# Softmax totals spread by way of DRAM, and the next sequence's last tiles normalised at other points, in an attention and top-1 LoRA block

## The chip, the cores and the metric

The kernel runs on one core of a Trainium2 chip. The metric is the device time of one execution in microseconds (us); lower is better. Before the change, three runs took 2750.57, 2753.59 and 2754.35 us, a median of 2753.59. One more execution was profiled; all traces and instruction times come from it.

The core's engines run their own instruction streams in order and wait for each other by semaphores: TensorE (PE, matmuls; its weight loads are listed apart as PEld), VectorE (DVE), ScalarE (ACT), GpSimd (POOL) and SyncE (SP). Every transfer of this kernel is issued on SP, in one order; an issue that waits holds back all issues behind it.

## What is computed

Four sequences of 1024 tokens with 1024 features, in fp32. One pre-norm block of attention with 32 heads of 32 features, then one pre-norm block that routes each token to the best of eight experts, each a LoRA pair of rank 16:

```python
def attn(x):                      # x is the layer norm of the input
    q, k, v = (split_heads(x @ w) for w in (wq, wk, wv))
    q, k = rotary(q), rotary(k)
    scores = einsum('bqhd,bkhd->bhqk', q, k) / sqrt(32)
    scores = where(causal, scores, lowest)
    return merge(softmax(scores) @ v) @ wo

def ffn(x):                       # x is the layer norm of what attention left
    logits = x @ route_w.T
    value, index = top_k(logits, 1)
    gate = one_hot(index, 8) * value
    h = einsum('bsd,erd->bser', x, A)
    return einsum('bser,eor->bso', gate[..., None] * h, Bw)

x = x + attn(layernorm(x))
x = x + ffn(layernorm(x))
```

## The kernel before

**Units.** The work is cut into 32 units u, one for each sequence b and each group g of four heads (128 columns of wq, wk, wv). A unit has 16 query tiles t of 64 queries; tiles 0 to 7 are its block 0, tiles 8 to 15 its block 1. While the scores of unit u are computed, the projections of unit u+1 are made and, from the second sequence on, one 128-token tile of the sequence before is finished: projected by wo, added, normalised, routed, and sent through its expert (`finish_steps`).

**Filling.** The program is written in the order that the engines take it. A list `SLOTS` gives a unit 11 slots: nine score rounds and two marks, "second" and "first", where the values are applied. Between the slots the steps waiting in `todo` are emitted, `do_some`, each with a cost; a step of cost 1 is one 128x512 matmul. The share of a slot is `ahead[r] / sum(ahead[r:ends_at])` (L1076 to L1081), where `ahead` is the list `LENGTHS` in units 0 to 6 and all ones later. `do_postponed` (L226) counts the cost of emitted steps and runs a postponed piece of work once its cost is used up.

**A score round** (`score_round`, L393) makes scores in PSUM for the query tiles of the slot (L406). There is one PSUM tile for this, `s` of the pool `ps_s`, and the value product uses the same one (L554). ScalarE copies the scores out (L417), GpSimd masks the diagonal (L420), DVE finds the maxima (L438), combines them (L459), ScalarE exponentiates with the sums (L467), and DVE transposes the probabilities in 32x32 squares (L492).

**Totals and values.** The keys of one query lie in two quarters of the partitions. `join_sums` (L525) runs when a block's probabilities are all transposed: four additions of a quarter and its partner (L534), one reciprocal of 128x16 (L535), and on GpSimd a copy that repeats each reciprocal 32 times (L537), so that `by` has 128x512 numbers with the queries on partitions. `apply` (L981) then multiplies probabilities and values on PE (L573), 64 or 128 matmul pairs, in one piece for block 0 and in two for block 1; between two pieces other steps are emitted and DVE transposes the value tile (`meanwhile`, L1028). `spread_sums` (L542) transposes `by` on PE with four matmuls (L547) and copies the result back on ScalarE (L548). `scale_values` multiplies the product by `by` on DVE (L593), which frees the PSUM tile for the next score round, and a later slot stores it to a DRAM scratch (L606). The mark "second" applies block 1 of the unit before, the mark "first" block 0 of the unit at hand. `join_sums` of block 1 comes in slot 1, that of block 0 in the rounds between the marks.

**Transfers.** Weights of the projections arrive in `w` (two buffers, L218), the values go to DRAM and come back in another layout (L507, L513), and wo, router and LoRA weights come as chunks (L647) into four buffers, the next three always ahead of the one in use.

**Change of sequence.** In units 7, 15 and 23 the next sequence's eight token tiles are loaded, normalised and transposed between other steps, by a `Norm` (L233): `load`; `find` (moments, L172 to L182: two BN_STATS, an aggregate, an addition on DVE and a power on GpSimd); `scale` (L186 on DVE); `turn` (eight PE transposes L198, two ScalarE copies L200 and L202). `change_steps` (L789) writes out by hand where tiles 2 to 7 stand among the steps of the last unit. For the second sequence, tiles 0 to 3 are turned in the steps of unit 6 and the rest in those of unit 7, all from buffers of the tag `row`; `scale(t)` there also finds the moments of tile t+1 (L270). For the third and fourth sequence not all tiles have a `row` buffer: tile 3 is loaded into the new unit's qT, tile 4 into its kT and tile 6 again into qT (L839), each before its rotary result is written there.

## Time and profile before

| what | value |
|---|---|
| median of three runs | 2753.59 us |
| the profiled execution's own time | 2747.7 us |
| its span, first to last instruction | 2745.9 us |
| mean granted TensorE clock | 0.998 |
| transfers | 317.86 MB, 16 DMA engines busy 41.6% on the kernel's queue |
| spreadings of totals (L547, four matmuls each) | 64 |
| reciprocals (L535) | 64, 253 ns each |
| products scaled (L593) | 128, 417 ns each; DVE idle before them 158.1 us in all |
| start of the first spreading, and of the last | 108.2 us, 2691.9 us |

A line of the groups reads: line, engine, operation, out<-in with their shapes, count | busy time and mean duration | idle time of that engine just before, and what ended it. Durations of neighbouring matmuls overlap, because they are pipelined: what one of them costs is the distance from start to start. In a timeline, a line is: start, duration, engine, line, operation, out<-in, count, and in brackets the idle time before it. Idle time of an engine which no other engine waits for costs nothing.

The waits of PE, longest sums first (us in total, times, longest):

```profile
PE pt_a L198 <- DVE x L186: 9.8, 2, 9.1
PE s L406 <- ACT pr L417: 7.2, 6, 1.7
PE pt_a L198 <- ACT yn L200: 5.2, 2, 2.6
PE pt_a L198 <- DVE qT L186: 4.5, 2, 2.3
PE po L690 <- DMA chunk<-in_wo: 4.0, 5, 1.7
```

The first of them is the start of the kernel, where the first tile is loaded and normalised. The chain of work that ended last lies for four fifths on PE:

```profile
PE 80%; DVE 14%; ACT 2%; DMA 1%; POOL 1%; issue 1%; SPq 0%; POOLq 0%; DVEq 0%; ACTq 0%
```

### The profile page before, as it was taken

The page shows a single profiled execution, that of the slowest core. Times are in us where ns is not written, and L with a number is a line of the kernel's source. Part 1 is how long each engine was busy: PE and PEld are TensorE (multiplying, and loading weights), DVE is VectorE, ACT ScalarE, POOL GpSimd, SP SyncE. Part 2 cuts the span into 40 slices and gives each one's busy share as a digit, 9 for nine tenths or more (in the row PEclk, how much of TensorE's full clock was granted, in tenths as well). Part 3 has the DMA queues.
Part 4 walks back from the last instruction along what each step waited for, and adds up shares of the span by engine and source line. Part 5 has one row for each costly group of instructions (what it writes and reads, how often), then busy time and mean ns, then how long its engine had stood idle before and what let it go on. Part 6 is the DMA issues. An engine that isn't in the chain of part 4 may idle for free.

```text
span 2745.9 us, 84082 instructions
## 1 busy us (share of the span) xinstructions
PE 2682.2 (98%) x35328; PEld 1322.0 (48%) x35328; DVE 2126.7 (77%) x4198; ACT 1755.0 (64%) x5033; POOL 638.1 (23%) x900
## 2 busy tenths in 40 slices
PE   8999999899999999989999999998999999999998
PEld 5444444444445444445444454444544444544445
DVE  4888889887777877887777778788777777778655
ACT  2877777876666676666666666666566666666521
POOL 2222223222222222222222222222222222222000
PEclk9999999999999999999999999999999999999999
DMA  3222232325444455551654444565255544446421
GB/s 118 52 56 56 56 94 56 78 56 150 131 135 114 121 141 142 151 171 43 175 145 122 135 110 121 149 165 146 63 157 150 138 128 128 115 119 196 129 67 55
DMA packets 448012, 317.86 MB, mean 116 GB/s; under 512 B 150289, under 2 KB 371729, under 8 KB 447633
## 3 DMA queue, kind: packets, MB, share of 16 engines
q1 hardware_dynamic: 447632, 312.47, 41.6%
q8 instruction: 278, 4.55, 0.7%
q14 instruction: 102, 0.83, 0.1%
HBM read 262.59 MB, written 49.81 MB: 114 GB/s over the span
## 4 chain that ended last, share of the span: by engine, by line
PE 80%; DVE 14%; ACT 2%; DMA 1%; POOL 1%; issue 1%; SPq 0%; POOLq 0%; DVEq 0%; ACTq 0%
PE po L690 14%; PE pq L313 14%; PE pk L313 13%; PE pv L313 12%; PE s L406 11%; PE av L573 9%; DVE top L438 4%; DVE pr L492 4%; PE ph L712 2%; PE pf L751 2%; DMA chunk<-in_wo 1%; DVE both L459 1%; PE pr L547 1%; ACT pr L417 1%; PE pt_f L198 1%
## 5 line engine op out<-in xcount | busy, mean ns | idle before, releaser
L467 ACT ACTIVATE pr<-pr,both 128x256 f32<-128x256 f32 (+15 forms) x2048 | 1045.1, 519 | 58.0 <-DVE both L459 57.9
L438 DVE TENSOR_REDUCE top<-pr 128x2 f32<-128x960 f32 (+15 forms) x768 | 651.1, 894 | 251.5 <-POOL pr L420 250.9
L417 ACT COPY pr<-s 128x640 f32<-128x640 f32 (+14 forms) x544 | 525.3, 1017 | 492.3 <-PE s L406 491.7
L492 DVE STREAM_TRANSPOSE pr<-pr 128x1024 f32<-128x1024 f32 (+11 forms) x768 | 664.3, 907 | 33.3 <-ACT pr L467 30.1
L420 POOL TENSOR_TENSOR pr<-pr,causal_sb 128x128 f32<-128x128 f32 x512 | 238.0, 472 | 1070.6 <-ACT pr L417 1062.4
L313 PE MATMUL pv<-xnT,wv 128*128 128x512 f32 x1024 | 484.1, 600 | 0.0
L313 PE MATMUL pq<-xnT,wq 128*128 128x512 f32 x1008 | 476.8, 600 | 0.6 <-ACT xnT L200 0.6
L313 PE MATMUL pk<-xnT,wk 128*128 128x512 f32 x1008 | 475.9, 601 | 0.0
L406 PE MATMUL s<-kT,qT 32*32 32x256 f32 (+4 forms) x17408 | 393.0, 385 | 10.7 <-ACT pr L417 7.2
L467 ACT ACTIVATION_READ_ACCUMULATOR pr<-pr,both 128x1 f32 x2048 | 400.8, 196 | 0.0
L690 PE MATMUL po<-chunk,attn 128*128 128x512 f32 x736 | 376.3, 597 | 4.0 <-DMA chunk<-in_wo 4.0
L406 PEld LDWEIGHTS s<-kT,qT 32*32 32x32 f32 x17408 | 187.2, 103 | 267.2 <-issue 101.8
L313 PEld LDWEIGHTS pk<-xnT,wk 128*128 128x128 f32 x1008 | 181.3, 190 | 234.8 <-issue 234.6
L313 PEld LDWEIGHTS pq<-xnT,wq 128*128 128x128 f32 x1008 | 182.6, 191 | 224.0 <-issue 221.8
L313 PEld LDWEIGHTS pv<-xnT,wv 128*128 128x128 f32 x1024 | 185.7, 190 | 217.2 <-issue 212.9
L573 PE MATMUL av<-pr,vals 64*32 64x256 f32 (+3 forms) x12288 | 273.2, 320 | 11.7 <-DVE pr L492 11.6
L573 PEld LDWEIGHTS av<-pr,vals 64*32 64x32 f32 x12288 | 215.5, 106 | 119.9 <-issue 54.5
L459 DVE TENSOR_TENSOR both<-top 32x4 f32<-32x4 f32 (+3 forms) x1152 | 213.4, 185 | 23.7
L690 PEld LDWEIGHTS po<-chunk,attn 128*128 128x128 f32 x736 | 135.2, 190 | 168.0 <-issue 149.6
L548 ACT COPY by<-pr 128x512 f32<-128x512 f32 x64 | 37.5, 586 | 260.5 <-PE pr L547 260.5
L593 DVE TENSOR_TENSOR at<-av,by 128x256 f32<-128x256 f32 x128 | 48.1, 417 | 158.1 <-ACT by L548 158.0
L690 PE MATMUL po<-wo,attn 128*128 128x512 f32 x256 | 116.7, 597 | 0.0
(87 smaller groups left out, 1705.8 us busy)
## 6 DMA issues: line engine op xcount, KB each, us to landing
chunk<-in_wo SPq DMA_DIRECT2D x368, 256.0 KB, 3.6
vals<-vd SPq DMA_DIRECT2D x256, 128.0 KB, 4.5
x<-in_x SPq DMA_DIRECT2D x58, 512.0 KB, 6.0
wq<-in_wq SPq DMA_DIRECT2D x32, 512.0 KB, 4.0
wk<-in_wk SPq DMA_DIRECT2D x32, 512.0 KB, 4.0
wv<-in_wv SPq DMA_DIRECT2D x32, 512.0 KB, 4.2
vd<-vT SPq DMA_DIRECT2D x128, 128.0 KB, 4.8
out_y<-x SPq DMA_DIRECT2D x32, 512.0 KB, 2.8
```

Of the source, the lines that this page charges most:

```text
L313: nc.tensor.matmul(at["p"], lhsT=wt[:, c, :], rhs=xnTs[b, tb][:, c, :], start=(c == 0), stop=(c == NC - 1),)
L406: nc.tensor.matmul(sc[i * SQ : (i + 1) * SQ, h, at : at + w].rearrange("p (j k) -> p j k", k=SQ), lhsT=of_q[rows, 2 * t + half], rhs=of_k[ ...
L417: nc.scalar.copy(pr[:, :, k0 : k0 + w], sc[:, :, at : at + w])
L420: nc.gpsimd.tensor_tensor(diagonal, diagonal, causal_sb.unsqueeze(1).to_broadcast([P, HG, SQ]), ALU.add)
L438: nc.vector.tensor_reduce(top[:, k, h : h + step], places[u, t][:, h : h + step, :], AX.X, ALU.max, negate=True,)
L459: nc.vector.tensor_tensor(dst[rows], src[rows], src[other], op)
L467: nc.scalar.activation(pr[:, h, :], pr[:, h, :], AF.Exp, bias=tops[u, t][:, h : h + 1], accum_out=dens[u, t // QT][:, t % QT, h : h + 1],)
L492: nc.vector.transpose(pr, pr)
L573: nc.tensor.matmul(avs[half][h * HD : (h + 1) * HD, t0:, :], lhsT=v[rows, j, h * HD : (h + 1) * HD], rhs=rhs, start=(j == 0), stop=(j == n ...
L690: nc.tensor.matmul(st["po"], lhsT=lhsT, rhs=rhs, start=(c == start), stop=(c == stop))
L712: nc.tensor.matmul(ph, lhsT=st["ynT"][:, c, :], rhs=w[:, c - i * RA, :], start=(c == 0), stop=(c == NC - 1),)
L751: nc.tensor.matmul(pf, lhsT=st["whT"], rhs=rhs, start=True, stop=True)
```

## The change

It has two parts.

*Totals.* `join_sums` writes the additions and the reciprocal into a constant tile `rec_sb` with 32 columns for each block (the unused ones are zeroed once), transposes it in 32x32 squares on DVE, and sets up two pieces of work, `put` and `get`. `put` stores four pieces of 16 rows x 32 numbers to a DRAM tile in which the 512 reciprocals of a head lie one after the other; `get` loads for each of the four heads its 512 numbers 32 times, once for each partition of the head in `by`. They are postponed by 2.0 and 5.0 of emitted cost; `spread_sums` runs what is left of them. GpSimd's copy, the four PE transposes and ScalarE's copy are gone.

*Changes of sequence.* For the second sequence (units 6 and 7), `scale` finds the next moments only for tiles 0 to 3, and the steps of unit 7 turn tile 4 after four projection steps, tile 5 after nine, then find, scale and turn tiles 6 and 7, the last of them after step 15. Unit 7 fills its slots by `LENGTHS`, but with 6.5 for each of the first two slots. For the third and fourth sequence tile 2 is turned one projection step and one held step later, tile 6 is loaded into kT when tile 4 has been turned, and tiles 5 to 7 are found, scaled and turned after other steps than before.

```diff
+LONG = 6.5
...
+    rec_sb = const.tile([P, 2, SQ], F32, name="rec_sb")
+    nc.vector.memset(rec_sb, 0.0)
...
-                if self.b == 1:
+                if self.b == 1 and k < TB:
                     self.find(k + 1)
...
-        den = dens.pop((u, blk)).rearrange("p (t c) h -> p c t h", c=2)
-        rec = small.tile([P, TB, HG], F32, tag="rec", name=f"rec_{u}_{blk}", bufs=2)
+        den = dens.pop((u, blk)).rearrange("p (t c) h -> p c h t", c=2)
+        rec = rec_sb[:, blk, : HG * TB].rearrange("p (h t) -> p h t", t=TB)
...
-        nc.vector.reciprocal(rec, rec)
-        bys[u, blk] = by = big.tile([P, TB, P], F32, tag="by", name=f"by_{u}_{blk}")
-        nc.gpsimd.tensor_copy(
-            by.rearrange("p t (h d) -> p t h d", d=HD),
-            rec.unsqueeze(3).to_broadcast([P, TB, HG, HD]),
-        )
+        nc.vector.reciprocal(rec_sb[:, blk, : HG * TB], rec_sb[:, blk, : HG * TB])
+        turned = small.tile([P, SQ], F32, tag="recT", name=f"recT_{u}_{blk}", bufs=2)
+        nc.vector.transpose(turned, rec_sb[:, blk])
+        there = dram.tile([HG * TB, P // SQ, SQ], F32, tag="recs", name=f"recs_{u}_{blk}")
+        by = big.tile([P, TB * P], F32, tag="by", name=f"by_{u}_{blk}")
+
+        def put():
+            for i in range(P // SQ):
+                nc.sync.dma_start(there[:, i], turned[i * SQ : i * SQ + HG * TB])
+
+        def get():
+            for h in range(HG):
+                of_h = there[h * TB : (h + 1) * TB]
+                nc.sync.dma_start(
+                    by[h * HD : (h + 1) * HD],
+                    bass.AP(of_h.tensor, of_h.offset, [[0, HD], [1, TB * P]]),
+                )
+
+        left = [put, get]
+        bys[u, blk] = by, left
+        for cost in (2.0, 5.0):
+            postponed.append([cost, lambda: left and left.pop(0)()])
...
-        by = bys.pop((u, blk))
-        pt = bank([P, TB, P], f"pr_{u}_{blk}")
-        for i in range(TB):
-            nc.tensor.transpose(pt[:, i, :], by[:, i, :], eye_sb)
-        nc.scalar.copy(by, pt)
-        return by.rearrange("p t k -> p (t k)")
+        by, left = bys.pop((u, blk))
+        while left:
+            left.pop(0)()
+        return by
...
-            out += [*h[:2], turn, *h[2:4], find(3), p[0], h[4], turning(2), h[5], p[1], route, scaling(3)]
+            out += [*h[:2], turn, *h[2:4], find(3), p[0], *h[4:6], p[1], turning(2), route, scaling(3)]
...
-            out += [p[6], find(5), p[7], turning(3), scaling(5), *p[8:10], turning(4), *p[10:12]]
-            chains = weave(chains[:-6], p[12:]) + chains[-6:]
-            out += [*chains[:2], find(6), *chains[2:4], scaling(6), turning(5), *chains[4:6], find(7)]
-            out += [*chains[6:8], scaling(7), turning(6), *chains[8:14], turning(7)]
-            return out + chains[14:]
-        out += [*chains[:2], turning(4), scaling(6), *chains[2:6], turning(5), scaling(7)]
-        out += [*chains[6:11], turning(6), *chains[11:16], turning(7)]
+            out += [p[6], find(5), p[7], turning(3), scaling(5), *p[8:10], turning(4)]
+            chains = weave(chains[:-6], p[10:]) + chains[-6:]
+            out += [*chains[:5], turning(5), find(6), *chains[5:7], scaling(6), *chains[7:9], find(7)]
+            out += [chains[9], turning(6), *chains[10:12], scaling(7), *chains[12:15], turning(7)]
+            return out + chains[15:]
+
+        out += [*chains[:4], turning(4), *chains[4:9], turning(5), *chains[9:11], norm.finding(6)]
+        out += [*chains[11:13], scaling(6), chains[13], norm.finding(7), chains[14], scaling(7)]
+        out += [turning(6), chains[15], turning(7)]
...
-                norm = Norm(b + 1, {0: (2,), 2: (5,), 3: (6,)}, {3: "q", 4: "k", 6: "q"})
+                norm = Norm(b + 1, {0: (2,), 2: (5,), 4: (6,)}, {3: "q", 4: "k", 6: "k"})
...
-            ahead = LENGTHS if not b and u + 1 < NG else [1.0] * ends_at
+            ahead = [1.0] * ends_at
+            if not b:
+                ahead = LENGTHS if g + 1 < NG else (LONG, LONG, *LENGTHS[2:])
```

In the steps of `change_steps`, `chains` are the projection steps of the next unit, `p` the wo steps of the tile that is finished, `h` the held last projection steps of the unit at hand, `turn`, `route`, `turn_hidden` and `adapt` the later stages of a finished tile.

## The prediction

> **What bounds the kernel now.** I read the engine totals first, then the windows of 50 us, the group of each instruction that goes, the waits of TensorE (PE), and last the timeline around the places that the change touches. Units are numbered u0 to u31, eight to a sequence; "apply (u, 0)" and "apply (u, 1)" are the value products of a unit's two blocks, each followed by one spreading of totals, 64 in all.
>
> ```profile
> PE 2682.2 (98%) x35328; PEld 1322.0 (48%) x35328; DVE 2126.7 (77%) x4198; ACT 1755.0 (64%) x5033; POOL 638.1 (23%) x900
> ...
> 200.00:250.00 50.00, 48.71 (x783) 23.11 (x782) 39.75 (x81) 37.56 (x117) 15.63 (x20) 1.00 0.28 65
> 1000.00:1050.00 50.00, 50.00 (x776) 25.98 (x774) 38.99 (x76) 30.80 (x91) 10.19 (x17) 1.00 0.41 107
> 1150.00:1200.00 50.00, 46.93 (x691) 25.62 (x691) 47.36 (x97) 35.02 (x93) 12.59 (x21) 1.00 0.51 160
> ...
> L547 PE MATMUL pr<-eye_sb,by 128*128 128x128 f32 x256 | 42.2, 287 | 0.9 <-issue 0.9
> ...
> PE av L573 <- DVE pr L492: 11.6, 2, 9.1
> ```
>
> The columns of a window are its stretch, its length, busy PE, weight loads, VectorE (DVE), ScalarE, GpSimd, clock, DMA share. From about 600 us on PE has no gap at all in most windows: there a PE instruction that goes is worth its time. In the first sequence PE idles about 1 us in 50 and DVE is close behind. At the changes of sequence (1150 and again 1850) DVE has 47 of 50 us and PE idles. The largest single wait, 9.1 us, stands at the first change, in u7.
>
> **The transposes that go (L547, with GpSimd's L537 and ScalarE's L548).** The steady unit, on PE, DVE and SP:
>
> ```profile
> 1028.64 3.68 PE L573 MATMUL av<-pr,vals 64*32 64x256 f32 x128
> 1035.03 2.35 PE L573 MATMUL av<-pr,vals 64*32 64x256 f32 x128
> 1037.31 0.66 PE L547 MATMUL pr<-eye_sb,by 128*128 128x128 f32 x4
> 1037.80 1.02 PE L690 MATMUL po<-chunk,attn 128*128 128x512 f32 x2
> ...
> 1027.98 0.25 DVE L535 RECIPROCAL rec<-rec 128x16 f32<-128x16 f32 x1
> 1038.67 0.76 DVE L593 TENSOR_TENSOR at<-av,by 128x256 f32<-128x256 f32 x2 [2.99 <-ACT by L548]
> ...
> 1020.13 8.98 SPq L647 DMA_DIRECT2D chunk<-in_ra  x3
> 1038.86 2.19 SPq L647 DMA_DIRECT2D chunk<-in_wo  x4
> ```
>
> The durations overlap, so I take starts: four transposes hold PE from 1037.31 to 1037.80, 0.49 us, and not 4 x 0.287. All 64 would be 31.4 us. ScalarE's 37.5 us (64 copies of 586 ns) and GpSimd's 39.1 us lie beside PE's work and are put at nothing; L593 waited for that copy, but ends 3.75 us before PE's next score round.
>
> **What takes their place.** One DVE transposition of 128x32, four stores of 2 KB, four loads of 64 KB, all on SP's queue; loads wait for the stores to land, and everything that SP issues later waits too. The smallest transposition in the trace, 128x128, takes 304 ns and 128x256 401, so 128x32 is estimated at 0.25; it falls into DVE's idle time before L593 (1.2 to 3 us) and costs nothing, as does one memset at the start, ahead of the first x. On SP the first of a row of issues takes 0.33 us, the next 0.45, so the fourth starts 1.35 after the first. For the landing the trace bounds both ends:
>
> ```profile
> chunk<-in_ra SPq DMA_DIRECT2D x24, 136.0 KB, 2.2
> vals<-vd SPq DMA_DIRECT2D x256, 128.0 KB, 4.5
> vd<-vT SPq DMA_DIRECT2D x128, 128.0 KB, 4.8
> ```
>
> Both new kinds are smaller than any of these, so I take the row nearest in packets, the first: 0.25 + 1.35 + 2.2 + 1.35 + 2.2 = 7.4 us from the reciprocal to the spread tile. The slow rows give 0.25 + 1.35 + 4.8 + 1.35 + 4.5 = 12.3. A trip faster than 7.4 gains only in u0, below.
> The Trainium skill, "DMA: Bandwidth & Descriptors", section "Bandwidth", speaks against such traffic: it counts transfers under 64 KB as dominated by descriptors. Its section "Anatomy of one DMA" has a fixed 2.0 us and bytes at 436 GB/s (measured from GpSimd's queue); with these the trip is an estimated 7.1 us, and the sum below would end 0.3 us better; the 2.2-us row decides.
>
> **Last three sequences.** In the steady unit the product ends 9.1 us after the reciprocal (1028.23 to 1037.31) in block 1, 9.3 in block 0. A trip of 7.4 is hidden; even at 12.3 L593 would end 13.1 after the reciprocal, and the next score round, which needs its PSUM, starts at 1043.18, that is 14.5 after it once 0.49 is gone. So 0.49 counts in full. What SP holds back: as built, in block 1 the stores stand before the second router load (ra) and the loads of totals before the third, and they wait for a reciprocal that ends at 1028.23, where SP before issued the third ra load at 1028.74. Stores are out at 1030.2, ra 2 follows at once, totals' loads at 1032.4 to 1034, ra 3 at 1034.2, landing 2.2 later at 1036.4; PE wants it at about 1039.4. In block 0 two weight chunks slip by 4 to 5 us and are used 13 and 18 us after the reciprocal: hidden. If this cover were gone, PE would wait at L712 or L690. Exceptions are the first block of u16 and u24, where a chunk is wanted 5.2 us after the reciprocal and lands at 1.9 + 3.6 = 5.5: 0.3 lost, twice. Sum: of the 48 spreadings, four are at changes of sequence; 44 x 0.49 = 21.6, less 0.6, is **21.0 us**.
>
> **First sequence.** Here DVE sets part of each unit:
>
> ```profile
> 238.08 0.25 DVE L535 RECIPROCAL rec<-rec 128x16 f32<-128x16 f32 x1
> 243.72 2.37 DVE L492 STREAM_TRANSPOSE pr<-pr 128x1024 f32<-128x1024 f32 x2
> 246.01 0.72 DVE L593 TENSOR_TENSOR at<-av,by 128x256 f32<-128x256 f32 x2
> 279.89 0.76 DVE L593 TENSOR_TENSOR at<-av,by 128x256 f32<-128x256 f32 x2 [2.78 <-ACT by L548]
> ```
>
> In block 0 L593 starts without idle time, 7.7 us after the reciprocal, inside a stretch in which DVE is busy from 239.5 to 277 and releases the next product; PE's 0.49 there becomes a wait. A trip of 7.4 just fits; each us above 7.7 is lost once per unit. In block 1 PE sets the pace, 0.49 counts, and L593 would have to start later than 10.4 after the reciprocal to hurt. So u1 to u6 give 6 x 0.49 = 2.9. In u0 the reciprocal ends at 106.78 and L593 starts at 109.54: no lead. With 7.4 it starts at 114.2, 4.7 us later, and DVE, which then runs without a pause to the next product at 135.18, carries that on: **-4.7**. First sequence without u7: **-1.8**.
>
> **Change of sequence, u7.** Before, tiles 6 and 7 are normalised ahead of the last probability transpositions (ended 548.6), for which PE waits from 539.0:
>
> ```profile
> 543.24 0.81 DVE L186 TENSOR_SCALAR x<-x,mv_a,rstd_a 128x1024 f32<-128x1024 f32 x1
> 543.97 1.28 DVE L175 BATCH_NORM_STATS2 st_a<-x 128x6 f32<-128x512 f32 x2
> ...
> 548.09 5.90 PE L573 MATMUL av<-pr,vals 64*32 64x256 f32 x128 [9.05 <-DVE pr L492]
> ...
> 543.00:548.00 5.00, 0.00 (x0) 0.00 (x0) 4.88 (x11) 4.70 (x17) 1.80 (x4) 0.50 0.01 2
> ```
>
> The wait is 9.05 us, and the clock fell to half, so the product took 5.90 instead of 3.68. After: the moments of 6 (1.7), scaling of 6 (0.8) and moments of 7 (1.7), 4.2 us, come behind; and LONG puts 6 more steps of 0.9 us ahead of the product. DVE waited 3.4 us at L593 near 514, of which 2.2 go, and the score round at 527.5 moves up as much; so the transpositions end near 548.6 - 4.2 - 2.2 = 542.2, and PE arrives near 539.0 - 2.2 + 5.4 = 542.2: no wait. But tile 6 is now turned between the two pieces of the product. DVE needs after the transpositions 1.0 (totals), 0.25, 2.9 (maxima L438, L459), 1.5 (swap), 1.7 (moments of 6), 1.2, 1.2 (vT), 0.8 (scaling), 10.6 us; PE has 3.7 + 1.8 = 5.5 us of work: a new wait of 5.1 us. PE alone gains 9.05 + 2.2 + 1.0 (two spreadings) - 5.1 = 7.1; but DVE arrives at the next score round only some 5 us early, and it follows PE closely to the end of the unit. I take **+5.5**, with 1 to 11 as ends (1 if the clock falls again and DVE holds the rest, 11 if the new wait closes).
> The Trainium skill, "TensorE: Matmul & The Clock Gate", section "What's actually happening", halves the clock after one idle window of about 3.4 us; by it the 5.1-us wait would cost an estimated 1.7 us more. The trace is not so clean: a gap of 2.60 us before 135.18 was followed by a window with clock 0.66, one of 2.60 at 1182 by none.
>
> **Changes at u15 and u23.** PE waits 2.6 (second tile), 0.5, 0.7, 1.6 (a chunk) and 2.3 (tile 6 in qT), 7.6 us each. The first is moved past the score round, but DVE ends the transpositions for the product at 1194.2 either way, so PE waits there instead. SP now holds three chunks, issued at 1190.3 to 1191.5 before, behind stores that wait for the reciprocal at 1195.23; the first is issued near 1197 and lands at 1199.5 to 1200.6 where PE wants it at 1197.9: 2 to 3 us lost. Later the 1.6 goes, since no projection step stands there any more, and the 2.3 shrinks to nothing or stays, because tile 6's load now waits for tile 4's turn and stands behind the value stores. I take **+1.1** each with their two spreadings, ends -4 and +4.
>
> **Sum.** 21.0 - 1.8 + 5.5 + 2.2 = 26.9, say 27. The profiled execution, 2747.7 (span 2745.9), would become 2720.7; it lies 5.9 below the median of the runs, 2753.6, which becomes **2726.6**.
>
> **Rivals.**
> *A slow trip, faster all the same.* At 10 us, between the rows, block 0 of u1 to u7 loses 7 x 2.3 = 16 and u0 another 2.6: gain 8, 2745. For it: the stores are 128-byte rows, like those of vd. Against: vd has 64 times as many, and DMA share is 0.28 in this stage. Chance 0.17.
> *A trip so slow that the first sequence pays for everything.* At 12.3 us block 0 loses 7 x 4.6 = 32, block 1 7 x 1.9 = 13, u0 4.9 more: 27 - 50 = 23 slower, 2777. It decides from 10.7 us on (21 + 2 + 3.3 lost, against 27); slower by 0.2% from 11.1. For and against it: as above. Chance 0.08.
> *More than forecast.* The wait at tile 6 closes, the changes of sequence give +4 each, block 0 of the first sequence counts too (3): 27 + 5.5 + 5.8 + 3 = 41, 2712. DVE, shown as full there, speaks against it. Chance 0.15.
> *The change doesn't do what it says*, the trip lying open behind every product: only u0 is built so, where stores and loads are issued right beside the product; elsewhere they come 6 to 9 us ahead.
>
> **How the numbers follow.** Forecast 0.60, with its own range 2718 to 2736 from the ends of the changes of sequence. The range for 8 in 10, 2712 to 2745, takes in the third rival and the first up to its value. A measurement of this kernel tells 0.2%, 5.5 us, from no change. Slower by that: the second rival, 0.08; within it: 0.06 of the first rival, trips of 10.4 to 11.1; faster: the rest, 0.60 + 0.15 + 0.11 = 0.86.
>
> **What would show it.** PE starts within 0.1 us of each product's end with a projection step; a steady unit shortens by 0.99 us from 82.33 (995.75 to 1078.08 for the spreading of block 0). The spread tile lands 7 to 8 us after the reciprocal. In the first sequence L593 of block 0 has no wait for a DMA except in u0, of some 7 us. In u7 the 9.1 us is gone and a wait at L198 of about 5 stands. At u15 PE waits for a wo chunk behind the first piece. Waits of L690 or L712 for chunks in steady units would prove me wrong, and so would L593 waiting on the totals' DMA in every unit.

## The result and the profile after

Predicted were 2726 us, with 2712 to 2745 as the range. Measured, 14 executions each on one chip: before 2750.8 us, after 2751.0 us (medians); ratio 1.0001, 95% interval 0.9993 to 1.0008. The change moved nothing that can be measured; the forecast of 27 us faster was wrong. The profiled execution of after took 2748.2 us (span 2746.4), that of before 2747.7. Among the executions of the variants below, one of `totals_alone` took 7545 us and stands in no ratio.

Line numbers below are those of the kernel named. In after, the join's additions are L539, the reciprocal L540, the transposition L542, the stores L548, the loads L553, the product L592, its scaling L612, a score round L410, the maxima L442 and L463, the turn of a tile L202 (copies L204, L206), its scaling L190, its moments L179 to L183, the value stores L511, tile 6's load L260, projections with wo L709, the router product L731. A kernel with lines added has its later lines as much further down.

From the page: engine total of PE, and the two new kinds of transfer with their size and median time from issue to landing.

```profile
PE 2672.7 (97%) x35072; PEld 1303.2 (47%) x35072; DVE 2146.2 (78%) x4263; ACT 1719.2 (63%) x4969; POOL 599.8 (22%) x836
...
by<-recs SPq DMA_DIRECT2D x256, 64.0 KB, 2.1
...
recs<-recT SPq DMA_DIRECT2D x256, 2.0 KB, 1.4
```

The 256 transpositions are gone and PE's busy time is 9.5 us less, while the span is 0.5 us longer: PE idles 10 us more. The waits of PE, of which the start of the kernel is 9.3 us, say where (us in total, times, longest):

```profile
PE pt_a L202 <- DVE x L190: 20.4, 5, 9.3
PE pt_a L202 <- DVE kT L190: 9.4, 2, 4.8
PE s L410 <- DVE at L612: 8.7, 3, 4.0
PE ph L731 <- ACT xnT L204: 7.6, 2, 4.1
```

The second and the fourth are new, the first has three more waits than before, and the third was 2.3 us in 2 there. The first two are turns of tiles at changes of sequence (and the start), the third are scalings that come late for a score round, the fourth is the router product at u15 and u23.

Where the time went is read best from one event that both kernels have 64 times, the start of the scaling of a product (L593 before, L612 after). After minus before, in us, from the two traces:

| scaling in | after − before | stretch up to it |
|---|---|---|
| u0, block 0 | +4.1 | lost |
| u4, block 1 | −3.5 | regained, and 0.4 for each spreading |
| u5, block 0 | +1.3 | 4.8 lost |
| u6, block 0 | 0.0 | partly regained |
| u7, block 1 | −4.1 | 4.1 gained at the first change |
| u14, block 0 | −9.0 | 4.9 gained, evenly |
| u15, block 1 | −0.3 | 8.6 lost at the second change |
| u22, block 0 | −5.2 | 4.8 gained, evenly |
| u23, block 1 | +3.2 | 8.3 lost at the third change |
| u30, block 0 | −2.2 | 5.4 gained, evenly |
| end of the span | +0.5 | 2.7 lost from there on |

Even gains in the steady units, and two falls at u15 and u23 that take back more than half of them. In detail, the steady unit, on PE, DVE and SP (start, duration, engine, line, operation, names, shapes, count, idle before):

```profile
1028.18 2.35 PE L592 MATMUL av<-pr,vals 64*32 64x256 f32 x128
1030.46 1.13 PE L709 MATMUL po<-chunk,attn 128*128 128x512 f32 x2
...
1021.18 0.25 DVE L540 RECIPROCAL rec_sb<-rec_sb 128x16 f32<-128x16 f32 x1
1030.59 0.76 DVE L612 TENSOR_TENSOR at<-av,by 128x256 f32<-128x256 f32 x2 [1.52 <-PE av L592]
...
1021.71 1.72 SPq L548 DMA_DIRECT2D recs<-recT  x4
1024.49 2.48 SPq L553 DMA_DIRECT2D by<-recs  x4
```

The scaling starts 0.06 us behind the product and waits for nothing else: the trip is hidden. But the pair of wo projections behind the product takes 1.13 us where it took 1.02 behind the transpositions, so 0.10 of the 0.49 us came back: a steady unit is 0.78 shorter, not 0.99. In before, the weight load of the first of the two starts at 1037.70, 0.11 ahead of its matmul at 1037.80, beside the last transposition; in after both start at 1030.46.

The second change of sequence, u15; the first line is the turn of tile 6 in before, the others are of after:

```profile
1228.94 1.06 PE L198 MATMUL pt_a<-eye_sb,qT 128*128 128x128 f32 x8 [2.26 <-DVE qT L186]
...
1223.14 1.94 PE L202 MATMUL pt_a<-eye_sb,kT 128*128 128x128 f32 x8 [4.60 <-DVE kT L190]
...
1234.94 1.87 PE L202 MATMUL pt_a<-eye_sb,x 128*128 128x128 f32 x8 [2.83 <-DVE x L190]
...
1216.66 2.35 DVE L442 TENSOR_REDUCE top<-pr 128x2 f32<-128x1024 f32 x2 [4.19 <-POOL pr L424]
1219.04 0.66 DVE L463 TENSOR_TENSOR both<-top 32x4 f32<-32x4 f32 x4
1219.73 1.29 DVE L179 BATCH_NORM_STATS2 st_a<-kT 128x6 f32<-128x512 f32 x2
1222.18 0.81 DVE L190 TENSOR_SCALAR kT<-kT,mv_a,rstd_a 128x1024 f32<-128x1024 f32 x1 [0.73 <-POOL rstd_a L185]
...
1206.51 6.91 SPq L511 DMA_DIRECT2D vd<-vT  x4
1213.52 0.64 SPq L260 DMA_DIRECT2D kT<-in_x  x1
```

PE waits 4.60 us for tile 6 and 2.83 for tile 7, where in before it waited 2.26 for tile 6 and not for tile 7. Tile 6's moments begin 0.03 us behind the maxima, which themselves waited 4.19 us for a masked score copy. And the clock fell: the eight transpositions took 1.94 us, where 1.04 is the duration of the same eight elsewhere.

### The profile page after: what moved, and what is told of

Its sections match the earlier page's. It is cut to its first block, busy times and chain, and to the rows that moved or that the text cites. A ratio compares the mean times of both kernels' runs of the same rounds, so it can differ in the third digit from the quotient of the medians.

```text
span 2746.4 us, 84059 instructions
## 1 busy us (share of the span) xinstructions
PE 2672.7 (97%) x35072; PEld 1303.2 (47%) x35072; DVE 2146.2 (78%) x4263; ACT 1719.2 (63%) x4969; POOL 599.8 (22%) x836
## 4 chain that ended last, share of the span: by engine, by line
PE 77%; DVE 15%; ACT 3%; DMA 2%; POOL 1%; issue 1%; SPq 1%; DVEq 0%; POOLq 0%; ACTq 0%
PE po L709 15%; PE pq L317 14%; PE pk L317 12%; PE pv L317 12%; PE s L410 11%; PE av L592 8%; DVE top L442 4%; DVE pr L496 4%; PE ph L731 2%; PE pf L770 2%; ACT pr L421 1%; DVE both L463 1%; ACT pr L471 1%; PE pt_f L202 1%; DMA by<-recs 1%
## 5 line engine op out<-in xcount | busy, mean ns | idle before, releaser
L442 DVE TENSOR_REDUCE top<-pr 128x2 f32<-128x960 f32 (+15 forms) x768 | 650.7, 894 | 265.4 <-POOL pr L424 264.8
L317 PE MATMUL pv<-xnT,wv 128*128 128x512 f32 x1024 | 489.9, 606 | 0.0
L410 PE MATMUL s<-kT,qT 32*32 32x256 f32 (+4 forms) x17408 | 395.8, 388 | 15.2 <-DVE at L612 8.7
L709 PE MATMUL po<-chunk,attn 128*128 128x512 f32 x736 | 380.8, 602 | 1.7 <-DMA chunk<-in_wo 1.6
L410 PEld LDWEIGHTS s<-kT,qT 32*32 32x32 f32 x17408 | 187.8, 103 | 274.5 <-issue 112.8
L592 PE MATMUL av<-pr,vals 64*32 64x256 f32 (+3 forms) x12288 | 271.1, 319 | 3.4 <-DVE pr L496 2.3
L592 PEld LDWEIGHTS av<-pr,vals 64*32 64x32 f32 x12288 | 212.4, 106 | 111.2 <-issue 64.2
L463 DVE TENSOR_TENSOR both<-top 32x4 f32<-32x4 f32 (+3 forms) x1152 | 207.5, 180 | 23.7
L709 PEld LDWEIGHTS po<-chunk,attn 128*128 128x128 f32 x736 | 135.5, 191 | 167.0 <-issue 148.7
L612 DVE TENSOR_TENSOR at<-av,by 128x256 f32<-128x256 f32 x128 | 48.2, 418 | 117.1 <-PE av L592 91.0
L355 POOL TENSOR_TENSOR qT<-qT,swapq 128x512 f32<-128x512 f32 x64 | 82.1, 1283 | 165.7 <-DVE swapq L351 165.7
L709 PE MATMUL po<-wo,attn 128*128 128x512 f32 x256 | 117.7, 601 | 0.0
```

Source lines behind the costliest of these rows:

```text
L317: nc.tensor.matmul(at["p"], lhsT=wt[:, c, :], rhs=xnTs[b, tb][:, c, :], start=(c == 0), stop=(c == NC - 1),)
L355: nc.gpsimd.tensor_tensor(dst[:, cols], dst[:, cols], other, ALU.add)
L410: nc.tensor.matmul(sc[i * SQ : (i + 1) * SQ, h, at : at + w].rearrange("p (j k) -> p j k", k=SQ), lhsT=of_q[rows, 2 * t + half], rhs=of_k[ ...
L442: nc.vector.tensor_reduce(top[:, k, h : h + step], places[u, t][:, h : h + step, :], AX.X, ALU.max, negate=True,)
L463: nc.vector.tensor_tensor(dst[rows], src[rows], src[other], op)
L592: nc.tensor.matmul(avs[half][h * HD : (h + 1) * HD, t0:, :], lhsT=v[rows, j, h * HD : (h + 1) * HD], rhs=rhs, start=(j == 0), stop=(j == n ...
```

## The experiments

Each ratio is to before on the same chip, since the medians of before differ by up to 2.5 us from chip to chip. 0.001 is 2.75 us.

| kernel | ratio | 95% interval |
|---|---|---|
| after | 1.0001 | 0.9993 to 1.0008 |
| totals_alone | 0.9970 | 0.9957 to 0.9982 |
| changes_alone | 1.0069 | 1.0056 to 1.0082 |
| no_late_changes | 0.9957 | 0.9942 to 0.9972 |
| no_first_change | 1.0005 | 0.9996 to 1.0015 |
| late_second_tile_back | 1.0010 | 1.0001 to 1.0018 |
| late_sixth_tile_back | 0.9955 | 0.9943 to 0.9968 |
| no_late_gpsimd_queue | 1.0077 | 1.0064 to 1.0091 |
| no_late_transposes_in_first | 0.9947 | 0.9935 to 0.9960 |
| sixth_load_left_out | 1.0007 | 0.9997 to 1.0016 |
| two_parts_together | 0.9946 | 0.9932 to 0.9959 |
| put_later_at_changes | 0.9946 | 0.9933 to 0.9958 |
| one_idle_transposition | 0.9976 | 0.9966 to 0.9986 |
| scaled_ahead_of_maxima | 0.9961 | 0.9946 to 0.9975 |
| scaled_ahead_and_transposes | 0.9943 | 0.9926 to 0.9960 |
| scaled_ahead_no_load | 0.9911 | 0.9897 to 0.9925 |
| sixth_load_first | 0.9913 | 0.9900 to 0.9927 |
| sixth_load_first_and_transposes | 0.9897 | 0.9883 to 0.9910 |

### The change in its parts

```diff
 totals_alone (from after) = its lines for the totals, and
-    change_steps, `k < TB` in scale, the tiles' homes, LONG
+    the same as before
 changes_alone (from before) = only these four as in after
```

> The totals go by way of DRAM, and the three changes of sequence stand as in the kernel before. Theory: the spreading pays and the changes at u15 and u23 took it back. From the shifts of the products in the trace of after, a steady spreading gives 0.39 us (48 of them 18.7), the first sequence up to u6 nothing on balance (its gains go at the first block of u5), the end loses 2: about 16 us faster, 2735. Rival, that the spreading itself gives nothing (its transfers hold up SP's queue and the other loads somewhere): 2746 to 2754. Second rival, my blind sum without u7's part (26.9 less 5.5 plus 1.0, less what u15 and u23 were to gain): 20 us faster or more, 2730 or less.

> The transposes on TensorE stay, and only the three changes of sequence are rearranged. Theory: u7 gains 3 to 4, u15 and u23 lose about 9.6 each: 16 us slower, 2767, with new gaps of about 4 us before the router product and before the turn of tile 6 at both late changes. Rival, that the changes are bad only because the totals' stores and loads stand in SP's queue there: within 4 us of before. The blind forecast (5.5 and 2 x 1.1 less the spreadings' part): 5 us faster.

Measured: 8 us faster (5 to 12), and 19 us slower (15 to 23). The rearranged changes cost 19 us by themselves, with no totals in SP's queue at all; that rival falls. In the trace of `changes_alone` (scalings against before, as in the table above) the stretches at u15 and u23 lost 11.3 and 10.4 us, and u7 gained nothing: its last scaling came 1.0 us later than in before. The totals alone gave half of the 16 us. The waits of PE in `totals_alone` show one reason:

```profile
PE po L709 <- DMA chunk<-in_wo: 13.4, 9, 3.4
```

Before, these waits were 4.0 us in 5. With the old order, chunks stand behind the totals' stores: 3.0 us at u15 and 2.0 at u23, as the prediction had it, and 3.4 at the start of u8, which it had not (there in this execution, not in after's; it took 2750.7 us, 8 above the median of `totals_alone`).

Then one change of sequence at a time was put back in after:

```diff
 no_late_changes: the branch "if p:" of change_steps, and
-    norm = Norm(b + 1, {0: (2,), 2: (5,), 4: (6,)}, {3: "q", 4: "k", 6: "k"})
+    norm = Norm(b + 1, {0: (2,), 2: (5,), 3: (6,)}, {3: "q", 4: "k", 6: "q"})
 no_first_change: the branch without p, "k < TB", and
-                ahead = LENGTHS if g + 1 < NG else (LONG, LONG, *LENGTHS[2:])
+            ahead = LENGTHS if not b and u + 1 < NG else [1.0] * ends_at
```

> The changed kernel with the changes of sequence at u15 and u23 put back as before (order and homes of the tiles), u7's kept. Theory: the 19 us that these two lost come back, 2732, and the half-clock windows near 1180, 1221, 1235, 1900 and 1914 are gone. Rival, that the loss at u15 and u23 comes from the totals' transfers there and not from the new order: no more than 5 us come back, 2746 or more.

> The changed kernel with u7's change put back as before (scaling of tiles 6 and 7 ahead, the old shares of steps), u15 and u23 as changed. Theory: u7's part gained 3 to 4 us in the changed kernel, so this is slower by that, 2754 to 2755. The blind forecast had 5.5 less one spreading, so 2756. Rival, that the steps of 6.5 in u7 push work out and gain nothing: 2751.

Without the late changes 12 us came back, of the 19 expected: u15 and u23 are the place of the loss, though the old order then pays for chunks (2.0 and 3.4 us of waits in its trace). u7's change is worth 1.1 us by this pair and 3.6 by `no_late_changes` against `totals_alone`; the intervals allow both. By the trace of `changes_alone` it is worth nothing without the totals, and why is open.

### Which part of the late changes

```diff
 late_second_tile_back (from after)
-    ... p[0], *h[4:6], p[1], turning(2), route, scaling(3)]
+    ... p[0], h[4], turning(2), h[5], p[1], route, scaling(3)]
 late_sixth_tile_back (from after): all lines of the branch behind this one, and the homes, as before
```

> The changed kernel, with one part of the changes at u15 and u23 put back: the second tile is turned before the score round again, not right before the router product. Theory: the router product then has a free bank, its gaps of 4.1 and 3.5 us and the half clock after them go, and a gap of 2.0 to 2.6 at the second tile takes their place: 1 to 2 us plus up to 3 of clock at each change, 4 to 8 us faster than after, 2743 to 2747. Rival, that the loss sits wholly in the sixth and seventh tiles: as after, 2749 to 2753.

> The changed kernel, with the other part put back: tiles 3 to 7 of these two changes in the old order, tile 6 loaded into the query buffer behind tile 3's turn; the second tile stays behind the score round. Theory: the gaps at tiles 6 and 7 (4.6 and 2.8 us) shrink to one of 2.3, so 5 us and 2 to 4 of clock at each change: 8 to 12 us less than after, less what the chunk waits of the old order give back (2 to 3 each, seen where all of it was put back): 2741 to 2748. Rival, that the wait of the router product is the larger part and stays: 2748 or more.

The second tile's place is worth nothing: the 4.1 us at the router product went, 1.9 at the second tile and 2.8 at a chunk came. The other part holds all of it: 12.7 us faster than after, as much as putting back both. The windows from the scaling in u14, block 0, to that in u15, block 0 (stretch, length, busy PE, weight loads, DVE, ACT, POOL, clock, DMA), of after and of `late_sixth_tile_back`:

```profile
1151.92:1256.89 104.97, 93.41 (x1144) 48.87 (x1143) 79.11 (x159) 61.51 (x170) 21.46 (x32) 0.92 0.49 138
```

```profile
1158.29:1254.98 96.69, 88.91 (x1144) 46.20 (x1143) 78.73 (x159) 61.23 (x170) 21.73 (x32) 0.98 0.52 150
```

The same 1144 matmuls: PE idles 11.6 us against 7.8, and is busy 93.4 us against 88.9. Of the 8.3 us, 3.8 are waits and 4.5 are PE busy for longer, at half clock. By the clock records after has five windows of 3.41 us at half clock here, which cost 6.7 us (half of PE's busy time in them): 2.5 behind the router product's wait, 4.2 behind those of tiles 6 and 7. `late_sixth_tile_back` has one, 1.7, behind the router product; before has none in this stretch.

### What holds tile 6

My prediction had named the load of tile 6, late behind the value stores.

```diff
 sixth_load_left_out (from after)
+                if t != 6:
                     nc.sync.dma_start(dsts[u], x[self.b, t * P : (t + 1) * P, :])
```

> The changed kernel without the load of tile 6 at u15 and u23: what the key buffer holds is normalised and turned in its place (the output of those rows is another). If the wait at tile 6 (4.6 us at 1218.5) comes from the load, which now stands behind the value stores in SP's queue, as my prediction had it, the wait goes here: 3 to 5 us and as much of clock at each change, 2738 to 2745. If it comes from VectorE's order (the moments of tile 6 start 0.03 us behind the maxima of the score round, without a wait for a DMA), nothing moves: 2749 to 2753, wait of 4 to 5 us still there.

The time is after's, and so are the waits:

```profile
1225.83 1.94 PE L202 MATMUL pt_a<-eye_sb,kT 128*128 128x128 f32 x8 [4.60 <-DVE kT L190]
...
1219.36 2.35 DVE L443 TENSOR_REDUCE top<-pr 128x2 f32<-128x1024 f32 x2 [4.19 <-POOL pr L425]
1222.43 1.29 DVE L179 BATCH_NORM_STATS2 st_a<-kT 128x6 f32<-128x512 f32 x2
```

So VectorE's order by itself makes the wait of 4.60. Next, only this order was moved:

```diff
 scaled_ahead_of_maxima (from after)
-    out += [*chains[:5], turning(5), find(6), *chains[5:7], scaling(6), *chains[7:9], find(7)]
-    out += [chains[9], turning(6), *chains[10:12], scaling(7), *chains[12:15], turning(7)]
+    out += [*chains[:5], find(6), scaling(6), turning(5), *chains[5:9], find(7), scaling(7)]
+    out += [chains[9], turning(6), *chains[10:15], turning(7)]
```

> The changed kernel, with only VectorE's order at tiles 6 and 7 of u15 and u23 moved: moments and scaling of tile 6 ahead of the maxima of the score round before its turn, scaling of tile 7 straight behind its moments, ahead of the next maxima; TensorE's order is as in after. Theory: the waits of 4.6 and 2.8 us come from these maxima, which stand in front and wait for ScalarE's copies; tile 6 then waits only for its load (issued at 1213.5, some 2.7 us of landing, then 1.7 and 0.8 of work: 1219, against TensorE's arrival at 1218.5), so both waits shrink to under 1 us and the half clock behind them goes: 13 to 16 us less than after, 2735 to 2738. Rival, that VectorE's maxima come as much later and the wait moves to the transpositions of probabilities or a score round: 5 us or less gained, 2746 or more.

> The same order, and block 0 of u0 to u6 spread by transposes. Theory: the two add, 1 to 3 us faster than the order alone: 2732 to 2736, at or below the best so far (2734). Rival, that block 0 of the first sequence is worth nothing (its earlier gain was within the interval): as the order alone.

11 us less than after, where 13 to 16 were expected. Tile 7's wait is gone; tile 6's is as long as before, for another reason:

```profile
1229.93 1.32 PE L202 MATMUL pt_a<-eye_sb,kT 128*128 128x128 f32 x8 [4.52 <-DVE kT L190]
1237.93 1.04 PE L202 MATMUL pt_a<-eye_sb,x 128*128 128x128 f32 x8
...
1226.40 1.29 DVE L179 BATCH_NORM_STATS2 st_a<-kT 128x6 f32<-128x512 f32 x2 [8.06 <-DMA kT<-in_x]
...
1212.57 8.15 SPq L511 DMA_DIRECT2D vd<-vT  x4
1220.81 0.64 SPq L260 DMA_DIRECT2D kT<-in_x  x1
```

Now the load is what tile 6 waits for, 8.06 us on DVE. Two causes stood in a row, and each hid the other. With block 0 of u0 to u6 spread by transposes on top (its edit is shown further down) it was 5 us faster still, with intervals that overlap.

Both causes away, once by leaving the load out, once with the load ahead of the value stores in SP's queue:

```diff
 sixth_load_first (from scaled_ahead_of_maxima)
-    if r in (second + 1, first_ + 1):
+    changes = b and b + 1 < B and g + 1 == NG
+    if r == first_ + 1 or r == second + 1 and not changes:
         for put in stores:
             put()
         stores.clear()
 ...
     fill(...)
+    if r == second + 1 and changes:
+        for put in stores:
+            put()
+        stores.clear()
```

> VectorE's order as in scaled_ahead_of_maxima, and the load of tile 6 at u15 and u23 left out (those rows' output is another). Theory: the wait at tile 6 has two causes in a row, VectorE's maxima and the late load, and either alone keeps it: taking one away gave 0.06 (load) and 0.35 % (order, all of it at tile 7). With both gone no wait over 1 us stands at tile 6 or 7: 3 to 5 us and 2 to 3 of clock at each change less than with the order alone (2742), 2728 to 2735. Rival, that a third thing holds the tile (its reciprocal deviation from GpSimd, ScalarE's copies): 2738 or more.

> The same order of VectorE, with the load kept and issued ahead of the value stores in SP's queue instead of behind them; nothing is left out. Theory: the load starts some 8 us earlier (1212.6 instead of 1220.8) and lands before VectorE comes to it, so as without the load: 2728 to 2736. Rival, that the value stores, now 1 us later behind the load, hold up the values' loads and a product: 2738 or more.

0.9911 and 0.9913: 24 us faster than before, and no wait at tile 6 or 7. The trace of `sixth_load_first`:

```profile
1220.03 1.04 PE L202 MATMUL pt_a<-eye_sb,kT 128*128 128x128 f32 x8
1226.42 1.04 PE L202 MATMUL pt_a<-eye_sb,x 128*128 128x128 f32 x8
...
1215.22 1.29 DVE L179 BATCH_NORM_STATS2 st_a<-kT 128x6 f32<-128x512 f32 x2 [1.84 <-DMA kT<-in_x]
...
1209.50 0.33 SPq L260 DMA_DIRECT2D kT<-in_x  x1
1210.40 6.00 SPq L511 DMA_DIRECT2D vd<-vT  x4
```

The load is issued 3.9 us ahead of the end of the maxima in front (1213.4), where in `scaled_ahead_of_maxima` it came 2.5 us behind it; DVE waits 1.84 us for it, and PE not at all. No product came to wait for the values. The waits at tiles 6 and 7 are settled: the late load and VectorE's order, and no third thing. The stretches that lost 8.6 and 8.3 us in after gain 3.0 and 3.2 against before in this trace, though the waits of some 4 us at the router product still stand in it (7.7 in 2); the second tile was not put back in this version.

### The first sequence, and the last spreading of a change

```diff
 no_late_transposes_in_first (from no_late_changes): join_sums and spread_sums
+    if u < 7 and blk == 0:   # additions, reciprocal, GpSimd's copy, transposes on PE and ScalarE's copy, as before
 put_later_at_changes (from that)
-        for cost in (2.0, 5.0):
+        for cost in (5.0, 8.0) if (u, blk) in ((14, 1), (22, 1)) else (2.0, 5.0):
```

> The version without the changes at u15 and u23 (2741 us), with block 0 of u0 to u6 spread by the old transposes again; all other spreadings by way of DRAM. Theory: in block 0 of the first sequence the trip has too little cover: u0 lost 4 us and u5 another 4 to 5 in the products' shifts, while the others gain 0.4 each: 2 to 6 us faster, 2735 to 2739. Rival, that the lost time is made up later in each unit anyway, since VectorE sets the pace: 2741 to 2744.

> The version with the old changes at u15 and u23 and transposes in block 0 of u0 to u6 (2734 us), where the totals' stores and loads of the last product before each of these two changes are issued 3 us of steps later. Theory: the weight chunks behind the stores in SP's queue come earlier, so that the waits for chunks there (3.5 and 2.0 us) and the half clock after them go; the product ends 11 to 12 us after its reciprocal and still hides the trip: 3 to 7 us faster, 2727 to 2731. Rival, that the chunks are late for another reason (their own landing, the queue's other stores): 2733 to 2736. Second rival, that the trip now lies open behind the product: 2736 or more.

> The two best parts together: tiles 3 to 7 of u15 and u23 in the old order with the second tile behind the score round (2737 us alone), and block 0 of u0 to u6 spread by transposes (2 us better where it was tried). Theory: the two are at different places and add: 2732 to 2736. Rival, that the gain of block 0 was a matter of how the clock's windows fell: 2737 to 2740.

Block 0 by transposes is 2.7 us better than without, with the loss in u5, block 0, gone from the trace, but the intervals overlap. Later stores and loads at u14 and u22 gave nothing: the waits for chunks went from 3.5 and 2.0 us to two of 1.0 and 2.0, and one of 1.4; inconclusive on the theory, and no gain. The two parts together took 2733.7 us, within the 2732 to 2736 expected of a sum, and 0.9946 is what 0.9955 less the 0.0010 of block 0 would give. But the intervals of the two parts overlap with it, so the sum is not shown; waits for chunks of up to 2.0 us remain. With the cause of the late changes removed it was:

> The same, and block 0 of u0 to u6 spread by transposes as before the change. Theory: both remedies add, 2 to 4 us less than sixth_load_first: 2725 to 2733, the best of the versions. Rival, that block 0 adds nothing: as sixth_load_first.

0.9897: 28 us faster than before and than after, median 2725.1 us, the best version of the study. The 4 us that it has over `sixth_load_first` are not resolved: the intervals overlap by 0.001.

### Another queue, and the 0.10 us

```diff
 no_late_gpsimd_queue (from no_late_changes), in put and get
-                nc.sync.dma_start(
+                nc.gpsimd.dma_start(
```

> The version without the changes at u15 and u23 (2741 us), with the totals' stores and loads issued by GpSimd instead of SP. Theory: SP no longer holds weight chunks behind the stores' wait for the reciprocal, so the waits for chunks at u15 and u23 (2.0 and 3.4 us) go with the clock they cost: 3 to 8 us faster than that version, 2733 to 2738. Rival, that the waits at u15 and u23 come from the shared DMA engines and not from the queue: 2741. Second rival, that GpSimd's own work behind its waits comes late, or that its issues are slower, so that products wait: over 2745.

33 us slower than `no_late_changes`, by the second rival. The waits for chunks went as the theory had it, from 6.1 us in 3 to one of 1.3, though with PE late everywhere this proves little about SP's queue. From its waits of DVE:

```profile
DVE at L612 <- DMA by<-recs: 112.5, 37, 8.0
```

In after these were 14.8 us. GpSimd spends 0.5 us on each of the 512 issues, and waits 166 us for transposed totals and 74 for the stores' landing with its own masks and rotations behind; the landings are slower too (2.2 and 2.6 us, against 1.4 and 2.1 from SP).

```diff
 one_idle_transposition (from no_late_changes), in spread_sums
+        if u > 7:
+            pt = bank([P, P], f"pr_{u}_{blk}")
+            nc.tensor.transpose(pt, eye_sb, eye_sb)
```

> The version without the changes at u15 and u23 (2741 us), with one transposition of the identity, whose result nobody reads, behind each product of the last three sequences. Theory: of the 0.49 us that went with four transpositions, 0.10 came back, because the first weight load of the next projection now lies open behind the product's small matmuls; the idle transposition takes that load's place and costs 0.11 less 0.10: 2740 to 2743, and the second matmul behind it starts 0.43 after the first instead of 0.53. Rival, that the transposition costs its full 0.11 on top: 48 times, 5 us slower, 2745 to 2748.

```profile
1033.99 2.35 PE L595 MATMUL av<-pr,vals 64*32 64x256 f32 x128
1036.28 0.33 PE L570 MATMUL pr<-eye_sb 128*128 128x128 f32 x1
1036.44 1.02 PE L712 MATMUL po<-chunk,attn 128*128 128x512 f32 x2
```

Behind one idle transposition the pair of projections takes 1.02 us again, so the 0.10 is what the first wide weight load costs behind the product's small matmuls, and something must take it. The transposition holds PE for 0.16 (1036.28 to 1036.44) and gives back 0.10: 0.06 net, 3 us for 48. The median steady spreading agrees, 0.07 longer than in `no_late_changes`, and 0.11 was the rival's. The time was 5 us up, at the rival's value, with intervals that overlap: it decides nothing, the trace does.

## Why the prediction was wrong, step by step

**The step that failed: changes at u15 and u23, "+1.1 each, ends −4 and +4".** They lost 8.6 and 8.3 us, though three spreadings' gain (1.2) lies in each of these stretches. It said of the wait at tile 6 that "the 2.3 shrinks to nothing or stays, because tile 6's load now waits for tile 4's turn and stands behind the value stores". The late load was seen and then priced at nothing, and the order of VectorE was not looked at: the moved steps `find(6)`, `scaling(6)` and `scaling(7)` had come to stand behind a score round's maxima, which wait for ScalarE and GpSimd, with two projections of work between on PE. What came were 4.60 and 2.83 us, and half clock. The half clock was no term of this step, and at u15 it cost 6.7 us, where before lost none. Nor did the 2.6 us at the second tile move to the product, as forecast: they became 4.1 at the router product (though putting that tile back alone gave no time). The weight chunk, "2 to 3 us lost", was there where the old order let it be seen (3.0), and hidden behind the router product's wait in after.

**Last three sequences, 21.0.** The mechanism was right: PE starts within 0.1 us of each product's end, trip and scaling are hidden, and no wait for a chunk in a steady unit of after is over 0.2 us. The size was off: 0.39 for each spreading instead of 0.49, as the weight load of the next projection lay beside the transpositions before. 44 x 0.39 = 17.2. Behind u30, block 0, another 2.7 went. Up to u30, block 1, it was 1.3: the tile landed 13.6 us after its reciprocal and the product had ended at 11.8. Between the two scalings of u31 it was 1.5, where after has a window at half clock (2665.2) and before none; `changes_alone`, without the totals' transfers, lost 1.7 there in the same way (see the last section). In between 1.0 was gained; the last 0.8, up to the end of the span, was not traced.

**The trip, 7.4 us.** Right: the spread tile landed 5.8 to 8.5 us after the reciprocal in the steady units, median 7.0, and 6.3 in u0, where the scaling waited 6.15 (forecast 7). Both slow-trip rivals fall.

**First sequence, −1.8.** The sum to u6 is 0.0, near it, by other terms. u0's 4.7 came (4.1) but was regained by u2, so "DVE carries that on" was wrong. And the claim that stores and loads come 6 to 9 us ahead "elsewhere" fails in u5, block 0:

```profile
447.24 1.60 PE L410 MATMUL s<-kT,qT 32*32 32x384 f32 x32 [4.02 <-DVE at L612]
...
435.41 2.29 DVE L539 TENSOR_TENSOR rec_sb<-den 32x16 f32<-32x16 f32 x4
446.33 0.76 DVE L612 TENSOR_TENSOR at<-av,by 128x256 f32<-128x256 f32 x2 [1.68 <-DMA by<-recs]
```

There the product ends 2.5 us after the reciprocal, the four additions took 2.29 us (0.75 in before), and the tile landed 8.1 us after the reciprocal: PE waits 4.02 us for the score round, where it waited 1.38 in before. The late tile accounts for 1.7 of the 4.8 us lost here. Another 2.6 had gone earlier in u5, where maxima waited 3.27 us for a masked score copy (0.67 in before); both are gone with block 0 spread by transposes, and why the second goes is open. Block 0 of u6 and of u7 waited for the totals too, 2.1 and 1.0 us, against the forecast of no such wait outside u0.

**u7, +5.5.** The waits came as drawn: 9.05 became 0.40, and 4.87 stand at tile 6's turn (5.1 forecast).

```profile
544.29 4.23 PE L592 MATMUL av<-pr,vals 64*32 64x256 f32 x128 [0.40 <-DVE pr L496]
555.30 1.49 PE L202 MATMUL pt_a<-eye_sb,x 128*128 128x128 f32 x8 [4.87 <-DVE x L190]
556.73 3.55 PE L592 MATMUL av<-pr,vals 64*32 64x256 f32 x128
```

The gain was 1 to 4 us in two pairs of runs, none in the trace of `changes_alone`, and 3.7 in the table for u7 with its two spreadings, as the 5.5 had them. The clock, taken as undisturbed, fell: 0.45 us on the eight transpositions (1.49 for 1.04) and 1.2 on the product (3.55 for 2.35), together the 1.7 that the Trainium skill's page "TensorE: Matmul & The Clock Gate" ("What's actually happening") would have added.

**Sum.** In the table 19.2 us are gained (4.1 at u7, 4.9 + 4.8 + 5.4 in steady units) and 19.6 lost (8.6 + 8.3 at the late changes, 2.7 at the end), with nothing either way up to u6. That the total came out at nothing is the chance of these sizes; the 0.06 that the prediction gave to a time within 5.5 us belonged to a slow trip, which did not come. A gain of the forecast's size came only with both causes at tile 6 taken away (2727.7 us without the load, 2725.1 in the best version).

## What to carry to other kernels

When a step of a queue is moved, list what it comes to stand behind on every engine that it uses, and price the wait of that neighbour, not only the step's own time. When one suspected cause is taken away and nothing changes, it isn't cleared: look for a second one in series, and take away both. A wait on PE of some 2 us or more can cost again in the clock behind it: 1.7 us for one window at half clock, 2.5 for the two behind tile 6.

## What the runs showed of the hardware

The clock of TensorE fell here without a wholly idle window. In 19 traces of this study the half-clock stretches are multiples of 3.41 us on one fixed grid in each trace. Laid on that grid, from 130 us on, of some 14,300 windows at full clock none with less than 1.59 us without a matmul was followed by half clock, and all with over 2.0 us were (between the two, 14 were and 62 were not); of 191 at half clock, the next stayed at half whenever more than 0.6 us were idle, and was full again whenever less than 0.48 were. After's windows behind tile 6 (columns as above, clock before the DMA share) show it:

```profile
1218.00:1221.40 3.40, 0.54 (x2) 0.00 (x0) 3.22 (x9) 1.01 (x5) 0.00 (x0) 1.00 1.02 218
1221.40:1224.80 3.40, 1.66 (x8) 1.69 (x9) 2.60 (x8) 0.54 (x1) 0.59 (x2) 0.50 0.78 124
1224.80:1228.20 3.40, 3.40 (x36) 0.69 (x34) 3.07 (x4) 1.27 (x6) 2.71 (x3) 0.50 0.00 0
1228.20:1231.60 3.40, 3.40 (x24) 1.44 (x8) 0.56 (x1) 2.88 (x8) 0.77 (x2) 1.00 0.00 0
```

Idle 2.9 of 3.4: half next. Idle 1.7 at half: half again. Busy throughout: full. So a wait of 2.4 us can cost 1.7 more or nothing, by where it falls on the grid. The turn of the last tile in u31 shows it, with the same wait in before (first) and in `changes_alone`:

```profile
2665.61 1.09 PE L198 MATMUL pt_f<-eye_sb,yn 128*128 128x128 f32 x8 [2.36 <-DVE yn L186]
...
2688.32 1.09 PE L200 MATMUL pt_f<-eye_sb,yn 128*128 128x128 f32 x8 [2.36 <-DVE yn L188]
```

In before a window of the grid begins at 2664.96, so the 2.36 us are split into 1.7 and 0.65, and the clock stayed full. In `changes_alone` they lie whole in the window from 2685.88 to 2689.29; the next one was at half clock, and 1.7 us went. In the same way the 2.60 us before 1184.96 in before, split at 1183.58, cost nothing. The grid isn't bound to the kernel's start: its first window begins 0.4 to 3.3 us after it in the 19 traces. That may also be why executions of one kernel differ by up to 9 us (2748 to 2757 for after); this was not tried.
